# A megakernel's last stage: fifteen weight buffers instead of thirteen, in the order in which memory comes free

## The chip, the cores and the metric

The kernel runs on one core of a Trainium2 chip. The time is the device time of one execution in microseconds. The kernel before took 4176.57 us, the median of three runs (4174.07 to 4178.53).

## The reference

Thirteen layers follow each other on 512 nodes with 768 features: four mixers (linear attention of several kinds), four graph layers on a graph of 8,704 edges, and four feed-forward layers, with a residual sum between them. All numbers are float32. The change lies in the last layer, a mixture of 16 experts in which each expert chooses its nodes, with shared experts beside them. For normalised nodes `xn` (512 x 768) it computes, in the form in which the kernel does it:

```
score = sigmoid(xn @ gate_weight.T)                 # 512 x 16
for each of 16 experts e:
    the 64 nodes with the highest score[:, e]       # 64 = 512 * 2 / 16
    h = silu(xn[chosen] @ Wg[e].T) * (xn[chosen] @ Wu[e].T)      # 64 x 3072
    x[chosen] += score[chosen, e] * (h @ Wd[e].T)
x += (silu(xn @ Ws_g.T) * (xn @ Ws_u.T)) @ Ws_d.T   # shared, 1536 hidden features
```

`Wg`, `Wu` and `Wd` hold 16 x 3072 x 768 numbers each. Together they are 453 MB, and each of them is read exactly once.

## The kernel before, in words

The whole network is one program. Feature matrices lie in SBUF node-major (`xn`, 128 nodes on the partitions, four groups `t`) or feature-major (`xnT`, 128 features on the partitions, six chunks `k`). `x` holds the residual stream. PE multiplies into PSUM, whose eight banks are handed out one at a time by `ps()` (line 238).

Instructions are written as a data flow on tiles. A planner, at build time, sets the order on each engine from the order of the text and from its own estimate of when the inputs of each instruction are there; it also adds all semaphores. `tc.issue_after(i)` puts the instructions of a block behind `i` on `i`'s engine and adds no wait on another engine. A tile of a pool takes the next of the pool's buffers and waits until all readers of the tile that had it are done. A pool that is opened on memory of a closed one waits in the same way for the tiles that lay there.

**Weights** come through SP's DMA queue in tiles of 128 x 2304 numbers, 1,152 KB each, by `w` (line 254; `wk` and `wr` are views of it). SP issues them strictly in order. No more than eight of these loads are under way at once, since each has one of eight semaphores. Up to the last stage they go through a pool `wp` of six buffers at the right end of SBUF. Small rows (biases) have a pool `rowp` beside it.

**The stage before** is `last_two` (line 1643): mixer and graph layer run interleaved. The mixer reads six qkv weight tiles (`m3_wqkv`) and then two projection tiles (`m3_wp`); the projection at line 1694 reads the tile `qk` and adds into `x`. As soon as a group of nodes is done, `norm1` normalises it into `xn`, and POOL writes it to memory as `there`, from which the experts' rows are fetched later. `to_fm` with `cut` (line 357) then transposes `xn` into `xnT`, three groups first and the last one when it is ready. The normalising square root on ACT (line 404) is kept as `self.root`.

**The last stage** is `ffn3` (line 1814).

- Line 1825 closes `wp` and `rowp`, and line 1826 opens a pool of 13 weight buffers, `f3_w`. By the sizes of the pools below it, this pool begins 64 bytes short of a multiple of 512 bytes, and so does each of its buffers.
- Experts are worked on in pairs `q` (eight of them), and each pair's 3072 hidden features in eight blocks `n` of 384. This makes 64 steps. A step `(q, n)` needs six weight tiles: two of `Wg` and two of `Wu` for `up` (line 1975) and two of `Wd` for `down` (line 1988). The two experts of a pair sit on 64 columns of PE each, side by side.
- The main loop (line 2039) does `up` of the next step and `down` of this one. `down` transposes `h` into `hT` and adds into two PSUM banks. After the last block of a pair they are copied to `outs`.
- `beside` spreads all other work over the steps: ranking the next pair (`rank`), choosing and fetching its rows (`choose`, `fetch`, `turn`), the way back (`way` makes the weighted selection `ohT`, `back` adds the outputs into `x`), and the twelve units of the shared experts (`shared`, `shared_down`). A unit of shared weights is three tiles `sw` of 384 KB that POOL loads into a pool of six buffers.
- The first pair has no earlier step to hide behind. Its ranking is `first_rank` (line 1859), once for each expert: PE spreads the scores over the partitions, ACT counts greater ones through `Sign` with an accumulator, and DVE counts equal ones in the right order. Then `shared(0, 0)`, `choose(0)`, `fetch(0)`, `shared(0, 1)` and `turn(0)` lead to the first `up`.

The mixtures `f0` and `f2` earlier in the network (`moe`, line 815) load their gate weights `wg` on ACT's queue at their own start (line 826).

Of the kernel before, what the change touches and what calls it, by code (L numbers as in the profile page):

```python
# [21 lines left out]
P = 128  # L22
# [148 lines left out]
class Net:  # L171
    def __init__(self, ctx, tc, dram, at, out):
        self.tc, self.nc, self.d, self.at, self.out = tc, tc.nc, dram, at, out
        nc = self.nc
        self.cw = ExitStack()
        self.wp = self.cw.enter_context(tc.tile_pool(name="wp", bufs=6, side="right"))
        self.keep = ctx.enter_context(tc.tile_pool(name="keep", bufs=1))
        self.small = ctx.enter_context(tc.tile_pool(name="small", bufs=4))
        self.rowp = self.cw.enter_context(tc.tile_pool(name="rowp", bufs=2, side="right"))
# [87 lines left out]
    def wk(self, ap):  # L267

        return self.w(ap).rearrange("p (k n) -> p k n", k=KC)
# [87 lines left out]
    def to_fm(self, x, out, cut=0):  # L357

        if cut:
            ps = [self.ps() for _ in range(KC)]  # L360
            for t in range(cut // P):
                for f in range(KC):
                    self.tr(ps[f][:, t * P : (t + 1) * P], x[:, t, f * P : (f + 1) * P])
            for f in range(KC):
                self.copy(out[:, f, :cut], ps[f][:, :cut])
            for f in range(0, KC, 3):
                p = self.ps()
                for k in range(3):
                    self.tr(p[:, k * P : (k + 1) * P], x[:, NT - 1, (f + k) * P : (f + k + 1) * P])
                self.copy(out[:, f : f + 3, cut:], p[:, :HW].rearrange("p (k n) -> p k n", k=3))  # L370
            return
        ps = [self.ps() for _ in range(KC)]
        for t in range(NT):
            for f in range(KC):
                self.tr(ps[f][:, t * P : (t + 1) * P], x[:, t, f * P : (f + 1) * P])
        for f in range(KC):
            self.copy(out[:, f, :], ps[f])

# [16 lines left out]
    def norm1(self, x, out, t):  # L395
# [10 lines left out]
        nc.vector.tensor_scalar(out[:, t, :], x[:, t, :], mv[:, 0:1], r, OP.subtract, OP.mult)  # L406
# [408 lines left out]
    def moe(self, f, act, xn, xnT, bs=None, fill=None, later=None):  # L815
# [6 lines left out]
        with ExitStack() as c:  # L822
            one = c.enter_context(tc.tile_pool(name=f + "_one", bufs=1))
            two = c.enter_context(tc.tile_pool(name=f + "_two", bufs=2))
            wg = one.tile([P, KC, 32], F32, name="wg")
            nc.scalar.dma_start(wg.rearrange("p k e -> p (k e)"), d[f + "_wg"])
# [987 lines left out]
    def ffn3(self, xnT, gate, there):  # L1814
# [5 lines left out]
        with ExitStack() as c:  # L1820
            two = c.enter_context(tc.tile_pool(name="f3_two", bufs=2))
            one = c.enter_context(tc.tile_pool(name="f3_one", bufs=1))
            sp = c.enter_context(tc.tile_pool(name="f3_s", bufs=6))

            self.cw.close()
            self.wp = c.enter_context(tc.tile_pool(name="f3_w", bufs=13))

            first = self.small.tile([P, 1], F32, name="r3")
            with self.tc.issue_after(self.root):
                nc.scalar.activation(first, self.eps, AF.Sigmoid)  # L1830
            io = one.tile([P, P], F32, name="io")
            nc.gpsimd.iota(io, pattern=[[1, P]], base=0, channel_multiplier=0, allow_small_or_imprecise_dtypes=True)
            number = self.number
            above = one.tile([P, NT, NX], F32, name="above")
            counted = one.tile([P, NX, NT, 3], F32, name="counted")
# [5 lines left out]
            side = one.tile([P, 7 * P], BF16, name="side")  # L1841
# [4 lines left out]
            loT = one.tile([P, N], F32, name="loT")  # L1846
# [12 lines left out]
            def first_rank(e):  # L1859
                p = self.ps()  # L1860
                for t in range(NT):
                    self.tr(p[:, t * P : (t + 1) * P], sc[:, t, e : e + 1].to_broadcast([P, P]))
                for t in range(NT):
                    junk = one.tile([P, N], BF16, name="sign")
                    i = nc.scalar.activation(junk, p, AF.Sign, scale=BIGGER, bias=low[:, t, e : e + 1],  # L1865
                                             accum_out=signs[:, t, e : e + 1])
                    junk = one.tile([P, N], BF16, name="junk")
                    nc.vector.scalar_tensor_tensor(junk, p, sc[:, t, e : e + 1], side[:, (3 - t) * P : (7 - t) * P],  # L1868
                                                   OP.is_equal, OP.mult, accum_out=sides[:, t, e : e + 1])
                return i  # L1870

            def rank(e):
# [4 lines left out]
                for t in range(NT):  # L1877
                    s = sc[:, t, e : e + 1]
                    for n, (a, b, op) in enumerate(((0, t * P, OP.is_ge), (t * P, N, OP.is_gt))):
                        if a < b:  # L1880
                            junk = one.tile([P, N], BF16, name="junk")
                            nc.vector.tensor_scalar(junk[:, a:b], p[:, a:b], s, None, op, OP.add,
                                                    accum_out=counted[:, e, t, n : n + 1])
                    junk = one.tile([P, N], BF16, name="junk")
                    nc.vector.scalar_tensor_tensor(junk[:, :P], p[:, t * P : (t + 1) * P], s, before, OP.is_equal, OP.mult,
                                                   accum_out=counted[:, e, t, 2:3])
                nc.vector.tensor_reduce(above[:, :, e : e + 1], counted[:, e], AX.X, OP.add)
# [3 lines left out]
            def choose(q):  # L1891

                oh = two.tile([P, NT, 2, CAP], BF16, name="oh")
                chosen[q] = oh, two.tile([P, KC, P], F32, name="xg")
# [4 lines left out]
            rows = {}  # L1899

            def fetch(q):
# [4 lines left out]
                sums = two.tile([P, 1], F32, name="sums")  # L1906
                nc.vector.tensor_reduce(sums, p[:, :2], AX.X, OP.add)
                who = two.tile([P, 1], I32, name="who")
                nc.vector.tensor_copy(who, sums)
# [35 lines left out]
            def shared(u, b):  # L1945
# [10 lines left out]
                if b == 0:  # L1956
                    nc.scalar.activation(h, p, AF.Silu)
                else:
                    nc.vector.tensor_mul(h, h, p)
# [199 lines left out]
```

## Time and profile before

| what | us |
| --- | --- |
| median of three runs | 4176.57 |
| the profiled execution, its own time | 4179.75 |
| its span | 4177.7 |
| first load of an expert weight issued | 3043.68 |
| first expert matmul | 3075.92 |
| last load of an expert weight landed | 4164.0 |
| PE busy, of the span | 4027.0 |
| expert matmuls, line 1981 | 567.6 |
| expert matmuls, line 1997 | 322.5 |

The profile is of one execution. Times in it are microseconds from the start of its span; the durations of single groups in the page are in nanoseconds. PE is the matrix engine and PEld its weight loads, DVE the vector engine, ACT the scalar engine, and POOL and SP issue DMAs here; POOL computes a little as well. A name like `SPq` is an engine's queue. `L1981` is line 1981 of the kernel before, and `ps<-w,xg` says that a matmul wrote PSUM from the tiles `w` and `xg`. A matmul in float32 appears as two records. The mean granted clock of PE over the execution was 0.989 of full speed.

### The profile page before, as it was taken

To read this page: it belongs to the slowest core of one execution; us is meant where nothing else is said; L and a number is where in the kernel's file an instruction comes from. 1 tells how busy PE (TensorE), PEld (TensorE's weight loads), DVE (VectorE), ACT (ScalarE), POOL (GpSimd) and SP (SyncE) were. 2 spreads that over 40 slices of the span, in tenths; PEclk is the share of its full clock that TensorE was granted. 3 is DMA by queue.
4 is the path that set the end of the run, shared out by engine and by line. 5 is a ranking of instruction groups with operands and counts; after the bars stand their busy time and mean duration, and the time that the engine had idled before them with its cause. 6 is when DMAs were issued, how large, how long until landed. Compare 5 with 4: busy or idle time off the path is not lost. (4 is left out here: it accounts for less than half of the span.)

```text
span 4177.7 us, 39229 instructions
## 1 busy us (share of the span) xinstructions
PE 4027.0 (96%) x16020; PEld 2066.7 (49%) x16061; DVE 1214.8 (29%) x2899; ACT 648.5 (16%) x1222; POOL 274.4 (7%) x329
## 2 busy tenths in 40 slices
PE   8989999999999999999999999999989999999998
PEld 3444555554455667655544444454644444444443
DVE  7721211113332147313411111126832122212211
ACT  1212000012222216311101010024510000000000
POOL 1120000010031010000000000020200000000000
PEclk9999999999999999999999999999999999999999
DMA  3210011121184011302211111082099999999998
GB/s 124 71 69 34 35 63 51 53 78 36 62 312 143 23 70 46 132 25 78 98 46 57 46 61 42 3 325 82 15 373 422 421 421 421 421 422 421 422 422 361
DMA packets 99548, 710.89 MB, mean 170 GB/s; under 512 B 12608, under 2 KB 12944, under 8 KB 29984
## 3 DMA queue, kind: packets, MB, share of 16 engines
q1 hardware_dynamic: 78064, 601.20, 36.0%
q0 software_dynamic: 16816, 95.80, 6.1%
q10 hardware_dynamic: 4480, 11.28, 0.7%
q8 instruction: 131, 2.15, 0.2%
q14 instruction: 57, 0.47, 0.0%
HBM read 685.68 MB, written 22.54 MB: 170 GB/s over the span
## 5 line engine op out<-in xcount | busy, mean ns | idle before, releaser
L1981 PE MATMUL ps<-w,xg 128*64 128x384 f32 x3072 | 567.6, 489 | 5.3 <-DMA w<-in_f_Wg_dram 3.0
L1981 PEld LDWEIGHTS ps<-w,xg 128*64 128x64 f32 x3072 | 235.3, 137 | 293.1 <-issue 264.1
L1601 PE MATMUL ps<-aT,w 128*128 128x512 f32 x864 | 372.3, 592 | 0.0
L1997 PE MATMUL ps<-w,hT 128*64 128x384 f32 x1536 | 322.5, 490 | 6.3 <-DMA w<-in_f_Wd_dram 2.9
L334 PE MATMUL ps<-xnT,w 128*128 128x512 f32 (+1 forms) x732 | 322.8, 598 | 0.2 <-ACT xnT L252 0.2
L1601 PEld LDWEIGHTS ps<-aT,w 128*128 128x128 f32 x864 | 164.2, 190 | 203.6 <-issue 202.3
L334 PE MATMUL ps<-w,xnT 128*128 128x384 f32 x672 | 222.7, 488 | 0.0
L334 PEld LDWEIGHTS ps<-xnT,w 128*128 128x128 f32 (+1 forms) x732 | 134.7, 185 | 176.3 <-issue 172.7
L1997 PEld LDWEIGHTS ps<-w,hT 128*64 128x64 f32 x1536 | 132.5, 136 | 171.8 <-issue 146.5
L411 DVE TENSOR_TENSOR x<-x,ps 128x384 f32<-128x384 f32 x224 | 123.4, 553 | 263.7 <-PE ps L334 193.0
L334 PE MATMUL ps<-C,parts 128*128 128x512 bf16 x843 | 187.8, 380 | 3.5 <-DVE inv L1623 2.4
L334 PE MATMUL ps<-w,hT 128*128 128x384 f32 x552 | 184.6, 490 | 2.6 <-ACTq L1056 1.7
L334 PEld LDWEIGHTS ps<-w,xnT 128*128 128x128 f32 x672 | 127.7, 191 | 88.8 <-issue 5.8
L1611 DVE TENSOR_TENSOR aT<-inv,ps 128x512 f32<-128x512 f32 x72 | 49.4, 686 | 365.7 <-PE ps L334 365.7
L1984 ACT ACTIVATE h<-ps 128x384 f32<-128x384 f32 x64 | 31.4, 490 | 788.9 <-PE ps L1981 788.9
L516 PE MATMUL ps<-ohd,so 128*128 128x512 bf16 x533 | 128.4, 391 | 21.1 <-DVE so L513 20.4
L1985 DVE TENSOR_TENSOR h<-h,ps 128x384 f32<-128x384 f32 x64 | 35.4, 554 | 376.8 <-PE ps L1981 376.8
L334 PEld LDWEIGHTS ps<-w,hT 128*128 128x128 f32 x552 | 103.1, 190 | 80.1 <-ACT xbT L252 7.1
L334 PE MATMUL ps<-w,aT 128*128 128x384 f32 (+1 forms) x416 | 139.6, 486 | 0.5 <-DVE aT L250 0.4
L334 PE MATMUL ps<-xnT,sw 128*128 128x512 f32 x288 | 139.6, 616 | 0.0
L334 PEld LDWEIGHTS <-parts 128*128 128x128 bf16 x864 | 84.8, 98 | 108.1 <-issue 8.9
L334 PE MATMUL ps<-w,nodesT 128*128 128x384 f32 x384 | 129.1, 486 | 0.0
(507 smaller groups left out, 4634.7 us busy)
## 6 DMA issues: line engine op xcount, KB each, us to landing
w<-in_f_Wg_dram SPq DMA_DIRECT2D x128, 1152.0 KB, 22.2
w<-in_f_Wu_dram SPq DMA_DIRECT2D x128, 1152.0 KB, 22.2
w<-in_f_Wd_dram SPq DMA_DIRECT2D x128, 1152.0 KB, 22.2
w<-in_g_w_dram SPq DMA_DIRECT2D x54, 1152.0 KB, 5.2
w<-in_m_wqkv_dram SPq DMA_DIRECT2D x24, 1152.0 KB, 7.5
w<-in_g_t_dram SPq DMA_DIRECT2D x12, 1152.0 KB, 5.1
w<-in_m_wp_dram SPq DMA_DIRECT2D x8, 1152.0 KB, 5.1
ea<-in_edge_attr_dram SPq DMA_DIRECT2D x34, 256.0 KB, 2.7
```

The lines of the kernel that those rows point to most:

```text
L334: i = self.nc.tensor.matmul(out, a, b, start=n == 0, stop=n == len(pairs) - 1)
L411: self.nc.vector.tensor_add(xs, xs, p)
L516: nc.tensor.matmul(p, so[:, n, t * P : (t + 1) * P], ohd[:, j, :], start=j == 0, stop=j == EJ - 1)
L1601: nc.tensor.matmul(outs[nb * 3 + f], w[:, k, f * P : (f + 1) * P], xT[:, k, :], start=first and k == 0, stop=last and k == KC - 1)
L1611: nc.vector.tensor_mul(aT[:, f, :], inv[:, r, :], p)
L1981: nc.tensor.matmul(p[a * 64 : a * 64 + 64, :HW], xg[:, k, a * CAP : (a + 1) * CAP], ws[b][a][:, k, :], start=k == 0, stop=k == KC - 1)
L1984: nc.scalar.activation(h, pg[:, :HW], AF.Silu)
L1985: nc.vector.tensor_mul(h, h, pu[:, :HW])
L1997: nc.tensor.matmul(po[nb][a * 64 : a * 64 + 64, :HW], hT[:, f * P + a * 64 : f * P + a * 64 + 64], wd[a][:, f, nb * HW : (nb + 1) * HW], s ...
```

## The change

- The ring of weight buffers has 15 places instead of 13, in four pools, and tile `i` takes its place by `i % 15`: places 0 to 3, 9 and 10 are the six old buffers of `wp`, which stays open; 4 to 8 are a pool `early`; 11 and 12 a pool `tail`; 13 and 14 a pool `rest_` that takes `rowp`'s memory.
- All weight buffers begin on a multiple of 512 bytes. A pad of 480 bytes at the right end of SBUF (`edge`, which POOL clears at the start) and one of 64 (`room`) see to it.
- The tiles `oh`, `xg`, `rows`, `ohT` and `hs` lie in a pool `late`, opened first and so in the place of `xn`. To make room `hs`, `ohT`, `outs`, `hT` and `who` have one buffer instead of two, `sw` five instead of six, `counted` two experts instead of 16, and several early tiles share memory with later ones.
- `first_rank` becomes `first_ranks`: both experts at once, ACT on one PSUM bank and DVE on the other, then the other way round.
- `shared(0, 1)` is cut in the middle of its six products, and `fetch(0)` stands between its halves. `shared_down(0, ...)` follows at once, ahead of the main loop. `way(q)` moves by two steps. The sum in `fetch` writes integers itself.
- `to_fm` with `cut` becomes `to_fm_last`, which says which copies ACT and DVE do and places DVE's behind the last normalising. The early table load of `Sigmoid` on ACT goes behind ACT's last copy instead of behind the square root.
- The gate weights of the mixtures `f0` and `f2` are loaded before `moe` is called, on POOL's queue, into a pool of the caller.

```diff
         self.cw = ExitStack()
+        edge = self.cw.enter_context(tc.tile_pool(name="edge", bufs=1, side="right"))
+        nc.gpsimd.memset(edge.tile([P, 120], F32, name="edge"), 0.0)
         self.wp = self.cw.enter_context(tc.tile_pool(name="wp", bufs=6, side="right"))
...
-        self.rowp = self.cw.enter_context(tc.tile_pool(name="rowp", bufs=2, side="right"))
+        self.cr = ExitStack()
+        self.rowp = self.cr.enter_context(tc.tile_pool(name="rowp", bufs=2, side="right"))
...
+    def gate_of(self, pool, f):
+        t = pool.tile([P, KC, 32], F32, name=f + "_gate")
+        self.nc.gpsimd.dma_start(t.rearrange("p k e -> p (k e)"), self.d[f])
+        return t
...
+    def to_fm_last(self, x, out):
+        nc, cut = self.nc, (NT - 1) * P
+        ps = [self.ps() for _ in range(KC)]
+        for t in range(NT - 1):
+            for f in range(KC):
+                self.tr(ps[f][:, t * P : (t + 1) * P], x[:, t, f * P : (f + 1) * P])
+        for f in (0, 1, 3, 4):
+            i = nc.scalar.copy(out[:, f, :cut], ps[f][:, :cut])
+        with self.tc.issue_after(self.scaled):
+            for f in (2, 5):
+                nc.vector.tensor_copy(out[:, f, :cut], ps[f][:, :cut])
+        for f in range(0, KC, 3):
...
-            wg = one.tile([P, KC, 32], F32, name="wg")
-            nc.scalar.dma_start(wg.rearrange("p k e -> p (k e)"), d[f + "_wg"])
...
+            late = c.enter_context(tc.tile_pool(name="f3_late", bufs=2))
             two = c.enter_context(tc.tile_pool(name="f3_two", bufs=2))
             one = c.enter_context(tc.tile_pool(name="f3_one", bufs=1))
-            sp = c.enter_context(tc.tile_pool(name="f3_s", bufs=6))
-            self.cw.close()
-            self.wp = c.enter_context(tc.tile_pool(name="f3_w", bufs=13))
+            tail = c.enter_context(tc.tile_pool(name="f3_m", bufs=2))
+            sp = c.enter_context(tc.tile_pool(name="f3_s", bufs=5))
+            c.callback(self.cw.close)
+            early = c.enter_context(tc.tile_pool(name="f3_w", bufs=5))
+            self.cr.close()
+            rest_ = c.enter_context(tc.tile_pool(name="f3_r", bufs=2))
+            self.taken = 0
+            def ring():
+                i, self.taken = self.taken % 15, self.taken + 1
+                return self.wp if i < 4 or 9 <= i < 11 else early if i < 9 else tail if i < 13 else rest_
...
+            def first_ranks():
+                ps = [self.ps() for _ in range(2)]
+                for e in range(2):
+                    for t in range(NT):
+                        self.tr(ps[e][:, t * P : (t + 1) * P], sc[:, t, e : e + 1].to_broadcast([P, P]))
+                for e in range(2):
+                    for t in range(NT):
+                        junk = two.tile([P, N], BF16, tag="h", name="sign")
+                        i = nc.scalar.activation(junk, ps[e], AF.Sign, scale=BIGGER, bias=low[:, t, e : e + 1],
+                                                 accum_out=signs[:, t, e : e + 1])
+                    for t in range(NT):
+                        junk = one.tile([P, N], BF16, name="junk")
+                        j = nc.vector.scalar_tensor_tensor(
+                            junk, ps[1 - e], sc[:, t, 1 - e : 2 - e], side[:, (3 - t) * P : (7 - t) * P],
+                            OP.is_equal, OP.mult, accum_out=sides[:, t, 1 - e : 2 - e])
+                return i, j
...
-            def shared(u, b):
+            def shared(u, b, between=None):
...
+                for k in range(KC):
+                    with tc.issue_after(i.ins) if i else nullcontext():
+                        i = nc.tensor.matmul(p, w[:, k, :], xnT[:, k, :], start=k == 0, stop=k == KC - 1)
+                    if between and k == KC // 2 - 1:
+                        with tc.issue_after(i.ins):
+                            i = between()
...
-                beside[8 * q + 2].append((way, q))
+                beside[8 * q + 4].append((way, q))
...
             with tc.issue_after(last.ins):
-                last = fetch(0)
+                last = shared(0, 1, lambda: fetch(0))
             with tc.issue_after(last.ins):
-                shared(0, 1)
+                for t in range(NT):
+                    shared_down(0, t)
             turn(0)
```

## The prediction

> **What bounds the kernel now.** I began with the time strip of the page: from the 30th of 40 slices on, the DMA engines stand at 9 tenths and move 421 to 422 GB/s, and PE stands at 9 too. So the last quarter, the stage that the change rewrites, is full on two resources at once. The table by stretches says the same in numbers (columns: stretch, length, busy time and count of PE, PEld, DVE, ACT, POOL, then granted clock, DMA share, GB/s):
>
> ```profile
> 3000.00:3050.00 50.00, 48.36 (x239) 32.70 (x238) 29.11 (x64) 15.37 (x27) 10.69 (x20) 1.00 0.31 110
> 3050.00:3100.00 50.00, 40.33 (x185) 18.80 (x185) 18.23 (x59) 10.16 (x23) 2.15 (x3) 0.90 1.01 418
> 3500.00:3600.00 100.00, 99.38 (x500) 44.28 (x496) 20.36 (x55) 6.03 (x12) 2.63 (x4) 1.00 1.01 422
> ```
>
> Before 3050 the DMA is nearly idle; afterwards it never rests. The list of what the load queue waited for between 2850 and 3082 us says why it starts so late (columns: waits in total, times, longest):
>
> ```profile
> SPq L258 <- DVE x L1796: 128.0, 1, 128.0
> SPq L258 <- PE ps L334: 78.8, 3, 41.5
> SPq L258 <- PE ps L1981: 14.5, 1, 14.5
> ```
>
> SP waits for memory: 128.0 us for the last addition of the graph layer, at about 3022, then for the last matmul of the mixer's projection, until the first load goes at 3043.68. Having filled 13 buffers it waits 14.5 us, from 3065.5 to 3080.0, for PE to finish with the first one.
>
> Which of the two bounds decides? I set each of the 384 weight loads' landing against the first matmul that uses it. Tile 6 landed 19.6 us before its use, tile 60 11.9 us, tile 144 5.4 us, tile 242 0.03 us, and from tile 368 on all wait. PE therefore begins with a stock, eats it for 700 us, scrapes the bottom near 3760, 3900 and 4037 and runs dry at 4122. The end shows it (start, length, instruction, in brackets the idle time before it):
>
> ```profile
> 4130.63 4.09 PE L1981 MATMUL ps<-w,xg 128*64 128x384 f32 x24 [1.49 <-DMA w<-in_f_Wg_dram]
> 4136.20 3.76 PE L1981 MATMUL ps<-w,xg 128*64 128x384 f32 x21 [1.01 <-DMA w<-in_f_Wu_dram]
> 4141.77 3.12 PE L1997 MATMUL ps<-w,hT 128*64 128x384 f32 x17 [0.83 <-DMA w<-in_f_Wd_dram]
> ```
>
> All such waits from 4122 on add up to 0.40+1.49+1.01+0.83+1.47+1.01+0.21+1.21 = 7.6 us. Both bounds must fall for the time to fall. Last I read the start of the stage:
>
> ```profile
> 3052.80 5.32 PE L334 MATMUL ps<-xnT,sw 128*128 128x512 f32 x12
> 3063.95 0.75 DVE L1868 SCALAR_TENSOR_TENSOR junk<-ps,sc,side 128x512 bf16<-128x512 f32 x1 [0.85 <-ACT sign L1865]
> 3065.43 0.75 PE L334 MATMUL ps<-number,oh 128*128 128x2 bf16 x4 [7.31 <-issue]
> 3066.04 8.20 PE L334 MATMUL ps<-xnT,sw 128*128 128x512 f32 x12
> 3074.72 0.87 PE L355 MATMUL ps<-ident,rows 128*128 128x128 f32 x6 [0.48 <-DMA rows<-f_there,who]
> 3075.92 7.96 PE L1981 MATMUL ps<-w,xg 128*64 128x384 f32 x48 [0.32 <-DVE xg L250]
> 3084.30 2.75 PE L334 MATMUL ps<-sw,hs 128*128 128x384 f32 x8
> ```
>
> PE has nothing for 7.31 us while ACT and DVE rank the first two experts, then computes the second half of shared unit 0 while the rows are fetched. The first expert matmul is at 3075.92; call that T0.
>
> **The change part by part.**
>
> *First ranks.* ACT and DVE took turns on the same PSUM bank, eight pairs from 3052.57 to 3064.71. The change gives each its own bank and lets them swap. The slower is DVE: 4 times about 0.8 us (0.75 and the read of the accumulator), twice, with a hand-over: 6.7 us from 3052.7, so 3059.4 instead of 3064.7, 5.3 us less. Then as before 0.4 for the sums and 0.9 for the one-hots: 3060.7. The separate cast (0.15 us) goes.
>
> *Order on PE.* Unit 0's first product ends at 3058.1, half of the second (2.66) at 3060.8, the matmuls of fetch follow (0.75), then the other half: 3064.2. The gather is issued at about 3062; with the 7.5 us that it took here under full DMA it lands at 3069.5, sooner if the queue is empty. Meanwhile PE does unit 0's down products, two groups like the one of 2.75 us, 5.5 us, after 0.8 us for the product on DVE: 3070.5. Turn 0.87 and copy 0.3: T0 is about 3071.5, **4.4 us earlier**. The down products formerly ran after T0: **5.5 us** of PE work leaves the stretch that PE fills without a pause.
>
> [...] The stretches of the clock:
>
> ```profile
> 3052.80:3058.20 5.40, 5.32 (x14) 2.10 (x12) 2.28 (x6) 2.84 (x8) 0.00 (x0) 1.00 1.01 428
> 3065.40:3074.30 8.90, 8.78 (x16) 3.62 (x16) 1.45 (x6) 0.43 (x1) 1.04 (x1) 0.65 1.01 419
> ```
>
> The same 12 matmuls take 5.32 us at clock 1.00 and 8.20 at 0.65, after the idle 7.31: 2.9 us lost. [...]
>
> *The loads.* Tiles 0 to 3 of the ring go to the old weight pool, whose buffers come free as blocks 2 to 5 of the mixer's qkv weights are done, at 2917, 2941, 2969 and 2996 by the trace. Tiles 4 to 8 lie where the graph layer lay (free at 3022), tiles 9 to 14 where the projection's weights, the qk tile and the bias rows lay (3043). Each tile takes 2.79 us when loads queue up, so nine are in by about 3042, with the first shared weights, and all 15 by about 3062. Before, about 10 tiles had landed at 3080.0, when PE gave back the first buffer, and 374 followed in 1084 us, to 4164.0. After, PE gives back the first at T0 + 4.1 = 3075.6 with 15 landed; 369 follow in 1084 - 5 x 2.79 = 1070 us, and the restart from an empty queue costs 5.2 - 2.8 = 2.4 us: the last lands at 4148. From there to the end 13.7 us as now: **4161.7 by DMA**.
>
> *By PE*: 4177.7 - 4.4 - 5.5 - 7.6 (waits that the stock now covers) = **4160.2**. The two nearly meet; the later decides, 4161.7.
>
> *Buffers on 512 bytes.* In the packet records a row of 9216 bytes takes a median of 349 ns in this stage, against 347 in the first MoE's gather and in loads to the old pool. [...] The loads to the old pool were off the line as well and yet took 347, so I take 2 in 349, at most 6 us, and as PE then decides at 4160.2 only 1.5 of it. Lower bound 0.
>
> *Gates of the other two MoEs.* They move from ACT's queue (0.35 us each) to POOL's (0.54), to an earlier place. POOL had been idle there for 46.8 us. In the first MoE this was late:
>
> ```profile
> 1160.24 3.59 PE L342 MATMUL ps<-xnT,wg 128*32 128x512 f32 x12 [2.20 <-DMA wg<-in_f_wg_dram]
> ```
>
> The last copy of xnT ends at 1159.4, and the first is ready by 1158.2, so 0.8 to 2.2 us come back, more if the clock stays up (3.59 us against 1.91 for such a group at full clock); the ranking on DVE behind it sets the gather. I take 1.5. In the second MoE, PE waited for xnT: 0.
>
> *Fewer buffers* for hT, outs, ohT, hs and who: 0. The next hT is copied about 5 us after PE's last use of the old one (3516.65 and 3521.5 in one step), which is the cover; without it each step would pay a copy of about 0.5 us, 32 us in all. For ohT the later place of way is the cover. Five shared buffers instead of six: POOL already waits 728.9 us for them, a whole unit ahead; the gathers behind these waits on POOL's queue come after the same PE work as before. Last-stage norm and copies: ACT's table load moves behind its copies, 0 to 0.3. The pad's memset at the start: 0.2 us on POOL, 0.
>
> **Sum** against the execution's own span: 4177.7 to 4160.2 (the DMA bound less 1.5 for the packets) less 1.5 for the first MoE: 4158.7, 19.0 us less. I keep 17, because two bounds that meet never fit step by step. The profiled execution's own time is 4179.75 (2.05 around its span), 3.2 above the median of 4176.57; the median less 17 is **4159.5**.
>
> **Rivals.**
>
> *The order on PE gets worse (slower).* PE's order is fixed at build time by a planner that guesses when loads arrive. Where it guesses late, it parts a pair of matmuls that would run side by side:
>
> ```profile
> 3499.74 4.73 PE L1981 MATMUL ps<-w,xg 128*64 128x384 f32 x26
> 3504.77 4.08 PE L1981 MATMUL ps<-w,xg 128*64 128x384 f32 x22
> ```
>
> That is 8.67 us on the chain instead of the 7.96 at 3075.92: about 0.65 us a break. Another plan could have more of them. Of 192 places (three pairs of tiles in 64 steps) perhaps half are broken now; to be slower by 0.2% the plan needs (17 + 8.4) / 0.65 = 39 more, then 4186. For: the plan is new from T0 on. Against: a fuller ring should make the planner wait less. Chance 0.12.
>
> *The loads don't start earlier (no change).* If one wait ahead of tile 0 on SP is still the projection's, the stream starts at 3043.7 as now, is never interrupted, and ends at 4164 whatever PE does: 4177.7 - 1.5, or 4175 on the median. SP is in order, so tile 4's memory at 3022 can hold back 9 to 14 too, without harm. With half of the early tiles: 4168. Against it: the blocks' ends at 2917 to 2996. Chance 0.13.
>
> *Both bounds fall further.* [...] Chance 0.11.
>
> **How the numbers follow.** The main forecast has 0.64, its own range 4151 to 4168. A change of 0.2%, 8.4 us, is about what a measurement of this kernel can tell from none. Faster: 0.64 + 0.11 = 0.75; same 0.13; slower 0.12. The range from 4149 to 4176 leaves out the slower rival and the low tail, some 0.17.
>
> **What would show it.** First ring loads at about 2917, 2941, 2969, 2996, five at 3022; DMA idle between about 3062 and 3075; no PE gap near 3060 and clock 1.00; T0 near 3071.5; first waits for weights later than 4122 or none. It is wrong if the stock is as small as before when the stream becomes steady, or if expert matmuls take more time in total than now.

## The result

The kernel after takes 4144.89 us (median of 4 runs, 4142.03 to 4147.45); the kernel before, run beside it, 4177.55 (4 runs, 4174.07 to 4179.18). The ratio is 0.9921, 95% interval 0.9908 to 0.9934. It is faster by 32.7 us. The forecast had the direction right and the gain at half its size: 17 us, 4159.5, with a range that ended at 4149.

The profiled execution of the kernel after spans 4142.6 us, 35.1 less than that of before. Its table by stretches, in the columns known from before (stretch, length, busy time and count of PE, PEld, DVE, ACT, POOL, granted clock, DMA share, GB/s):

```profile
3000.00:3050.00 50.00, 48.06 (x221) 30.92 (x221) 27.55 (x64) 16.39 (x38) 9.68 (x18) 1.00 0.70 284
3050.00:3100.00 50.00, 47.94 (x225) 21.68 (x225) 21.52 (x74) 4.47 (x8) 3.41 (x5) 1.00 0.83 332
3500.00:3600.00 100.00, 100.00 (x542) 45.10 (x542) 17.52 (x40) 6.04 (x12) 2.64 (x4) 1.00 1.01 427
```

Two things differ. The DMA is at work before 3050 (284 GB/s instead of 110) and rests afterwards; and when both kernels are in their steady state, at 3500, the same loads run at 427 GB/s instead of 422. What the load queue waited for between 2850 and 3082 (total, times, longest):

```profile
SPq L262 <- PE ps L338: 175.0, 8, 41.3
SPq L262 <- PE ps L2024: 40.7, 3, 28.7
SPq L262 <- DVE x L1814: 26.0, 1, 26.0
```

The wait of 128.0 us for the graph layer is 26.0 now. Single tiles go at 2908.9, 2932.7, 2960.0 and 2987.8, five at 3014.4 to 3016.5, six more up to 3036.9; then SP waits 28.7 us, to 3066.0, until PE gives back the first buffer. By the packet records all 15 tiles have landed when the first expert matmul begins; in the kernel before it was 9.7 of 13. The start of the stage:

```profile
3043.72 7.89 PE L1995 MATMUL ps<-xnT,sw 128*128 128x512 f32 x18
3051.45 0.40 PE L338 MATMUL ps<-number,oh 128*128 128x2 bf16 x4
3051.71 2.82 PE L1995 MATMUL ps<-xnT,sw 128*128 128x512 f32 x6
3055.38 5.43 PE L338 MATMUL ps<-sw,hs 128*128 128x384 f32 x16 [0.85 <-DVE hs L2002]
3060.64 0.82 PE L359 MATMUL ps<-ident,rows 128*128 128x128 f32 x6
3061.92 7.96 PE L2024 MATMUL ps<-w,xg 128*64 128x384 f32 x48 [0.46 <-DVE xg L254]
```

The gap of 7.31 us is gone, and 18 matmuls at a granted clock of 1.00 (3043.7 to 3051.4) fill its place. The end has two waits for weights instead of eight, 2.5 us instead of 7.6:

```profile
4112.28 4.09 PE L2024 MATMUL ps<-w,xg 128*64 128x384 f32 x24 [1.42 <-DMA w<-in_f_Wg_dram]
...
4117.94 3.76 PE L2024 MATMUL ps<-w,xg 128*64 128x384 f32 x21 [1.10 <-DMA w<-in_f_Wu_dram]
```

**Where the 35.1 us lie.** The work ahead of the last stage takes a time that differs by several us from run to run: the last matmul of the projection (the one that adds its bias; call its start P) lies at 3043.3 in the kernel before, but at 3033.4 in e6_start below, whose code is the same up to there. So two intervals are read instead of the span. From P to the end: 4177.7 - 3043.28 = 1134.4 us before, 4142.6 - 3034.74 = 1107.9 after, **26.5 less**. This interval repeats well: a second kernel with the last stage of before gives 1134.6, one with the stage of after in another load order 1108.1. And at the gate of the first MoE, from the start of the last six transposes of xn to the end of the gate product: 6.2 to 6.9 us in the seven kernels of this study with the old gate (6.7 in the profile before), 3.4 in all seven with the new one, **about 3 less**. The rest, some 5 us of the spans or 3 of the medians, is within the spread of the work ahead of P, so it is not counted as a gain of the change.

### The profile page after: what moved, and what is told of

The parts are those of the page before. It is cut to its first block, busy times and chain, and to the rows that moved or that the text cites. A ratio compares the mean times of both kernels' runs of the same rounds, so it can differ in the third digit from the quotient of the medians.

```text
span 4142.6 us, 39287 instructions
## 1 busy us (share of the span) xinstructions
PE 4014.0 (97%) x16061; PEld 2065.4 (50%) x16061; DVE 1212.9 (29%) x2890; ACT 648.9 (16%) x1223; POOL 276.7 (7%) x331
```

## The experiments

All times are medians, each beside runs of the kernel before on the same chip. "Landed" is the landing of the last weight tile, counted from P; "tail" is from there to the end of the span.

| kernel | us | before beside it | ratio, 95% interval | P to end | landed | tail |
|---|---|---|---|---|---|---|
| before | 4177.55 | | | 1134.4 | 1120.3 | 14.1 |
| after | 4144.89 | 4177.55 | 0.9921 (0.9908, 0.9934) | 1107.9 | 1093.8 | 14.1 |
| e1_align | 4166.92 | 4176.69 | 0.9974 (0.9963, 0.9985) | 1124.7 | 1108.2 | 16.6 |
| e2_nopads | 4161.31 | 4176.69 | 0.9965 (0.9952, 0.9979) | 1122.9 | 1108.7 | 14.2 |
| e4_ring13 | 4150.07 | 4176.69 | 0.9940 (0.9926, 0.9953) | 1113.4 | 1099.3 | 14.1 |
| e5_order | 4144.58 | 4176.69 | 0.9921 (0.9908, 0.9935) | 1108.1 | 1094.0 | 14.1 |
| e3_gates | 4169.29 | 4173.93 | 0.9993 (0.9984, 1.0002) | 1134.6 | 1120.3 | 14.3 |
| e6_start | 4171.83 | 4173.93 | 0.9996 (0.9987, 1.0005) | 1134.3 | 1120.2 | 14.1 |
| e1b_256 | 4162.57, one run | 4173.93 | | 1123.0 | 1107.8 | 15.2 |
| e1c_480 | 4173.20, one run | 4173.93 | | 1137.3 | 1123.2 | 14.1 |
| e7_both | 4162.72 | 4177.69 | 0.9964 (0.9951, 0.9978) | 1119.3 | 1105.3 | 14.0 |
| e1d_128 | 4174.84, one run | 4177.69 | | 1133.9 | 1119.8 | 14.2 |
| e9_late | 4179.79 | 4177.85 | 1.0005 (0.9995, 1.0014) | 1142.3 | 1128.2 | 14.1 |
| e10_noedge | 4148.55 | 4177.85 | 0.9926 (0.9909, 0.9943) | 1110.4 | 1096.3 | 14.1 |

The last column is worth more than it seems. In twelve of the fourteen the end follows the last landing by 14.0 to 14.3 us, the time that PE needs for what still hangs on the last tile. In those kernels the loads set the end. Only in e1_align (16.6) and its twin e1b_256 (15.2) had PE still other work to do when the last tile came.

**e1_align: the ring on 512 bytes, alone.**

```diff
 number = self.number
+one.tile([P, 16], F32, name="room")
 above = one.tile([P, NT, NX], F32, name="above")
```

> The kernel before with one unused tile of 64 bytes ahead of the ring's pool, so that the ring's buffers begin on a multiple of 512 bytes instead of 448 past one; nothing else. Theory (the beginning of the buffer sets the rate of the loads): loads at 427 GB/s instead of 422 between 3100 and 4100 us, the 9216-byte packet records near 348 ns in the mean instead of 352, the waits for weights after 4122 us gone or nearly so; PE's own work then bounds the stretch, so 6 to 12 us less than before. The prediction's term: 0 to 6 us less, 1.5 likeliest. Rival (the rate comes from the order of the loads, not from where the buffers begin): 422 GB/s still, and the time within 2 us of before.

Measured: 9.8 us less in the median, 9.7 from P to the end. The mean 9216-byte record from 3100 to 4100 takes 348.7 ns instead of 351.9. No wait for weights is left on PE, and the load queue spends its time differently. Its waits from 3060 to 4180 in the kernel before, and then in e1_align:

```profile
SPq L258 <- PE ps L1981: 273.5, 119, 14.5
SPq L258 <- DMA w<-in_f_Wg_dram: 188.1, 87, 4.8
SPq L258 <- DMA w<-in_f_Wu_dram: 166.4, 80, 3.7
SPq L258 <- DMA w<-in_f_Wd_dram: 164.3, 78, 3.9
SPq L258 <- PE ps L1997: 141.0, 64, 7.4
```

```profile
SPq L258 <- PE ps L1982: 601.2, 213, 15.6
SPq L258 <- PE ps L1998: 299.4, 115, 7.5
...
SPq L258 <- DMA w<-in_f_Wg_dram: 7.3, 3, 3.3
```

Before, SP waited 518.8 us for earlier loads and 414.5 for buffers; now it waits 900.6 us for PE to give buffers back. So the bound went from the loads to PE, and 1124.7 us is what PE needs with the old start of the stage.

The gain is larger than the visible waits. The steps of the two kernels begin at the same times after T0, to 0.02 us, up to the one at 817.8 us, so the pad makes nothing faster on PE itself. From there the kernel before falls behind by 10.0: by 1.1 at a stop of 0.27 us at 3904.3, which the prediction did not list, and by the rest at its eight stops from 4122 on. At each of these nine stops the matmul ahead runs out its full 0.49 us, where in an unbroken row the next one starts after 0.16 (48 of them take 7.96): 9 x 0.33 = 3.0, and with the waits of 7.9 us that is 10.9, near the 10.0. The theory holds; the prediction's term (1.5, at most 6) does not.

**e2_nopads: the kernel after without both pads.**

```diff
-edge = self.cw.enter_context(tc.tile_pool(name="edge", bufs=1, side="right"))
-nc.gpsimd.memset(edge.tile([P, 120], F32, name="edge"), 0.0)
...
-one.tile([P, 16], F32, name="room")
```

> The kernel after without its two pads (the 480-byte one at the right edge and the 64-byte one of the last stage): the five buffers of the early pool begin 448 past a multiple of 512 and those of the old weight pool 480 past one, as they did before. Theory: 422 GB/s again, and since the last loads of the kernel after land with 0 to 5 us to spare, the time rises by 8 to 12 us to about 4155. The prediction's term: 1.5 us more, at most 6. Rival (where buffers begin does nothing): within 2 us of the kernel after.

Measured: 16.4 us more than after in the median, 15.0 from P to the end; mean record 352.5 ns. The DMA summary from 3100 to 4100 of the kernel after, of e1_align and of e2_nopads:

```profile
DMA packets 53124, 426.96 MB, mean 427 GB/s; under 512 B 6125, under 2 KB 6125, under 8 KB 8238
```

```profile
DMA packets 52975, 425.18 MB, mean 425 GB/s; under 512 B 6126, under 2 KB 6126, under 8 KB 8366
```

```profile
DMA packets 52391, 420.58 MB, mean 421 GB/s; under 512 B 6063, under 2 KB 6063, under 8 KB 8239
```

426.96 to 420.58 is 1.5%. A tile of 128 rows of 9216 bytes takes 2.76 us at 427 GB/s, 384 of them 1060 us, and 1.5% of that is 16: the 15 us measured. (The 425 of e1_align is no slower DMA: it paused for buffers.) The theory said 8 to 12; it took the waits at the end for all the slack that would be lost, where in truth the loads are the bound throughout. This is the part of the gain that the forecast had counted at only 1.5 us: without the pads the kernel takes 4161.3, within 2 us of the forecast. That it comes so near is partly luck, since other terms were off too, in both directions (see below).

**e1b, e1c, e1d: which boundary?** The pad of e1_align with 320, 32 and 192 bytes, so that the ring begins 256, 480 and 128 past a multiple of 512.

```diff
-one.tile([P, 16], F32, name="room")
+one.tile([P, 80], F32, name="room")
```

(80 floats in e1b_256, 8 in e1c_480, 48 in e1d_128.)

> As the aligned version of before, but with 320 bytes of padding: the ring begins 256 past a multiple of 512. Theory 1 (what counts is a multiple of 512): 9216-byte records near 352 ns, 422 GB/s, as before. Theory 2 (what counts is a multiple of 256): near 348 ns, 425 to 427 GB/s, time near 4167. Theory 3 (only a multiple of 64 or less counts): would also hold for before, so no difference from it.

> As the aligned version of before, but with 32 bytes of padding: the ring begins 480 past a multiple of 512, where the old weight pool of the kernel before lies. If the prediction was right that loads to such a place run like aligned ones: near 348 ns and 425 to 427 GB/s. If it merely saw them under a lighter load: 352 ns or more in the mean, 422 GB/s or less.

> As the aligned version of before, but with 192 bytes of padding: the ring begins 128 past a multiple of 512. So far the mean 9216-byte record took 348.7 ns at 0, 348.8 at 256, 351.9 at 448 (192 past a multiple of 256) and 353.4 at 480 (224 past one). If the cost grows with the bytes past a multiple of 256: 350 to 351 ns here, 423 to 425 GB/s. If any start off a multiple of 256 costs the same: 352 to 353 ns, 421 to 422 GB/s. If 128 is enough: 348 to 349 ns.

The DMA summary from 3100 to 4100 of e1b_256 and of e1c_480:

```profile
DMA packets 52978, 425.20 MB, mean 425 GB/s; under 512 B 6126, under 2 KB 6126, under 8 KB 8366
```

```profile
DMA packets 52372, 420.31 MB, mean 420 GB/s; under 512 B 6070, under 2 KB 6070, under 8 KB 8254
```

Mean record and rate by where the ring begins: 0 past 348.7 ns, 256 past 348.8 ns (both 425 GB/s, limited by PE); 128 past 352.0 ns and 422; 448 past (before) 351.9 and 422; 480 past 353.4 and 420. So a multiple of 256 was enough here. Where a ring of thirteen on the line (a multiple of 512) is not held back by PE (e7_both), the mean is 347.5 ns; against that, a start off the multiple costs 1.3, 1.3 and 1.7%. It hardly grows with the bytes past it (128, 192, 224), so of the two descriptions in the last expectation the second is nearer. Each of the three places was run once, but the records behind a mean number over 44,000.

**e10_noedge: only the old pool off the line.**

```diff
-edge = self.cw.enter_context(tc.tile_pool(name="edge", bufs=1, side="right"))
-nc.gpsimd.memset(edge.tile([P, 120], F32, name="edge"), 0.0)
```

> The kernel after without the pad at the right edge alone: the six buffers of the old weight pool lie 480 past a multiple of 512, the other nine stay on one. From the last matmul of the projection to the end: after 1107.9 us, without both pads 1122.9. If each tile pays for where its own buffer begins: the six of fifteen take 353 ns a record, the others 347, 424 GB/s over all and 5 to 7 us more than after. If one misplaced pool slows all queues: near 1121. If the old pool's place does nothing, as the prediction held: 1108.

Measured: 2.5 us more than after from P to the end, mean record 348.3 ns, 426 GB/s: none of the three. Six of fifteen buffers lie 480 past the line, yet 91% of the records take 347 ns as if all were aligned. When all thirteen lay there (e1c_480), 6% did. The cost is therefore no fixed price of a record here. The packet records tell more when they are sorted by start and cut into tiles. The share of records of 350 ns or more, by place in the ring (0 to 3, 9 and 10 are the six off the line; the first 60 tiles are left out):

| place | 0 | 1 | 2 | 3 | 4 | 5 | 6 to 8 | 9 | 10 | 11 | 12 to 14 |
|---|---|---|---|---|---|---|---|---|---|---|---|
| % | 1 | 13 | 36 | 45 | 31 | 4 | 0 | 1 | 2 | 3 | 0 to 1 |

In a run of four loads off the line the slow records grow from tile to tile, and they are gone within two tiles on the line; a run of two shows hardly any. So in this kernel the time of a load hangs on the loads just ahead of it, and not only on where its own buffer begins. What lies behind that, no run shows.

**e4_ring13: two buffers fewer.**

```diff
-rest_ = c.enter_context(tc.tile_pool(name="f3_r", bufs=2))
-    i, self.taken = self.taken % 15, self.taken + 1
-    return self.wp if i < 4 or 9 <= i < 11 else early if i < 9 else tail if i < 13 else rest_
+    i, self.taken = self.taken % 13, self.taken + 1
+    return self.wp if i < 4 or 9 <= i < 11 else early if i < 9 else tail
```

> The kernel after with a ring of thirteen: the pool of two that takes the place of the bias rows is left out, all else is the same. Theory (the loads bound the end, so the stock at the start of the stage counts in full): two tiles of 2.76 us fewer are in when PE gives back the first buffer, so 5.5 us more than after, about 4150. Rival (PE's own work bounds it, the stock is ample): within 2 us of after, 4143 to 4147.

Measured: 5.5 us more from P to the end, 5.2 in the median. Two tiles are 2 x 2.76 = 5.5. Each of these two tiles, in hand before PE gives the first one back, counts in full.

**e5_order: the same buffers in the opposite order.**

```diff
-    return self.wp if i < 4 or 9 <= i < 11 else early if i < 9 else tail if i < 13 else rest_
+    return tail if i < 2 else rest_ if i < 4 else early if i < 9 else self.wp
```

> The kernel after with the same fifteen buffers taken in the opposite order, those that come free last first: no load can then start before about 3034 us, and fifteen tiles of 2.76 us take until about 3076. Theory: the loads never pause between 3034 and the end; the pause that the kernel after has before 3066 us, some 10 to 14 us, is lost, the end comes 8 to 12 us later, about 4154; the first expert matmul stays at 3062. Prediction's bound by loads said the same thing in its own numbers. Rival (PE bounds it): within 2 us of after.

Measured: no difference, 4144.58 us and 1108.1 from P. The edit did not hold the loads back as it was meant to. Its load queue (start, length, instruction):

```profile
2913.04 0.33 SPq L262 DMA_DIRECT2D w<-in_f_Wd_dram  x1
...
3018.53 0.80 SPq L262 DMA_DIRECT2D w<-in_f_Wg_dram  x2
```

A down tile goes first, at 2913. The planner sorts the loads by when their memory comes free, so the early start is the same, only with other tiles. So what counts is which memory the fifteen buffers use; the order in which the ring is written to run through them is worth nothing here.

**e9_late: the first fifteen loads held back.**

```diff
...
 i = self.nc.sync.dma_start(t[:parts, :n], ap)
+self.hold -= self.hold > 0 and (self.tc.add_manual_dep(i.ins, self.added.name, mybir.DependencyInfo(mybir.DependencyClass.Sync, mybir.DependencyReason.DATA), reason="late start") or 1)
...
-self.nc.vector.tensor_add(xs, xs, p)
+self.added = self.nc.vector.tensor_add(xs, xs, p).ins
...
-self.taken = 0
+self.taken, self.hold = 0, 15
```

> The kernel after with one wait more: the first fifteen loads of the ring wait for the last addition of the projection, so that none starts before the place where the loads of the kernel before began; ring, pads and the start of the stage are those of after. The planner, told of the wait, parts more pairs of expert matmuls while the loads are young. From the last matmul of the projection to the end the kernel after takes 1107.9 us. Theory (the loads bound the end, so each tile that is not in when PE gives back the first buffer costs its 2.76 us): about 11 of 15 tiles in, 8 to 11 us more, 1116 to 1119. Rival (the early start only fills buffers that PE does not need yet): 1108 to 1110.

Measured: all of the gain is gone, 4179.79 us and 34.4 us more from P. The wait sits later than intended, for by the time the loads are written down the last addition is that of shared unit 0's down products:

```profile
3064.46 0.80 SPq L261 DMA_DIRECT2D w<-in_f_Wg_dram  x2
```

That is 26.7 us after P, so 0 tiles are in where the kernel after has 15. The arithmetic still fits: 15 x 2.76 = 41.4 us of loading ahead, less the time that the kernel after stands still from there to its first free buffer (it goes on at 3066.03, 31.3 after P: 4.6 us), is 36.8 against 34.4 measured. Here the loads never pause: 26.7 from P to the first issue, 1101.5 to the last landing and a tail of 14.1 make up the 1142.3. PE waits 24.5 us for weights:

```profile
PE ps L2024 <- DMA w<-in_f_Wg_dram: 16.8, 9, 6.2
PE ps L2040 <- DMA w<-in_f_Wd_dram: 4.0, 6, 0.8
PE ps L2024 <- DMA w<-in_f_Wu_dram: 3.7, 7, 1.0
```

The 22 stops cost their lost overlap too: 24.5 + 22 x 0.33 = 31.8 us, against 2.5 + 0.7 in the kernel after. The 6 us that are left over on PE's side were not taken apart.

**e6_start: the new start of the stage alone.**

```diff
-rest = pieces[2:]
+rest = pieces[4:]
-for e in range(2):
-    last = first_rank(e)
+last, _ = first_ranks()
...
-    last = fetch(0)
+    last = shared(0, 1, lambda: fetch(0))
 with tc.issue_after(last.ins):
-    shared(0, 1)
+    for t in range(NT):
+        shared_down(0, t)
```

The definitions of `first_ranks` and of `shared` are those of the change.

> The kernel before with only the start of the last stage changed: each of the first two experts ranked in a bank of its own, the gather between the halves of shared unit 0's second product, and the unit's down products ahead of the first expert matmul. Theory: the first expert matmul comes 5 to 6 us earlier; the loads, which bound the end, stay as fast and only get their first buffer back 5 to 6 us earlier, so the end comes 5 to 6 us earlier, about 4171, and PE waits some 5 us more for weights near the end, where the moved products of 5.5 us now leave room. Rival (PE bounds the end): both terms count, 10 to 11 us less, about 4166. Rival (loads bound it and their start at 3043.7 decides): no change.

Measured: nothing, 1134.3 us from P against 1134.4. The third account is right: the loads bind, and their start decides. By the packet records they take 1119.8 us from the first issue to the last landing, in the kernel before 1119.9, and they never pause. When PE gives back its first buffer, 10.3 tiles of 13 have landed (11.0 before), so others are still under way, and a buffer that comes free earlier brings no load forward. T0 itself came 2.3 us earlier (30.4 after P instead of 32.6), less than the 5 to 6 expected: the rows were late behind the loads (1.41 us). PE waits for weights 14.6 us instead of 7.9.

**e7_both: the pad of e1_align and the new start of e6_start.**

```diff
+one.tile([P, 16], F32, name="room")
 above = one.tile([P, NT, NX], F32, name="above")
```

With it go all the edits of e6_start.

> The kernel before with the pad of 64 bytes and the new start of the last stage together; the ring keeps its thirteen buffers and its late start. From the last matmul of the projection to the end: before 1134.4 us, with the pad alone 1124.7, with the start alone 1134.3, after 1107.9. Theory (the loads hid what the start gains; once they are faster, PE bounds the stage and the start counts): 1113 to 1117, so 8 to 11 us less than with the pad alone; what is left to 1107.9, 6 to 9 us, is the earlier and larger stock. Rival 1 (the loads bound it again at once): 1120 to 1124. Rival 2 (the earlier stock does nothing): 1108 to 1110.

Measured: 1119.3 us from P, between the theory and the first rival: 5.4 less than with the pad alone, of 8 to 11 expected. PE's waits show why (3060 to 4180):

```profile
PE ps L2009 <- DMA w<-in_f_Wd_dram: 2.7, 3, 1.2
PE ps L1993 <- DMA w<-in_f_Wg_dram: 1.5, 1, 1.5
PE ps L1993 <- DMA w<-in_f_Wu_dram: 1.4, 3, 0.9
```

5.6 us of waits for weights are back and the tail is 14.0: as soon as PE had room the loads were the bound again, at their faster rate. From here to the kernel after it is another 11.4 us. Two tiles are 5.5 of them (e4_ring13); the other 5.9 are the earlier start of the loads together with all else that e7_both leaves out, not parted further.

**e3_gates: the gates alone.**

```diff
-wg = one.tile([P, KC, 32], F32, name="wg")
-nc.scalar.dma_start(wg.rearrange("p k e -> p (k e)"), d[f + "_wg"])
...
-net.moe("f0", AF.Gelu, xn, xnT, "f0_bs", fill=part)
+net.moe("f0", AF.Gelu, xn, xnT, net.gate_of(right, "f0_wg"), "f0_bs", fill=part)
```

The same is done for `f2`.

> The kernel before with the gate weights of the first and second MoE loaded from GpSimd's queue before the MoE begins, as the kernel after does; nothing else. Theory (the gate was late by more than the wait of 2.2 us shows, because the product also ran at a lowered clock): the gate product takes 2.25 us instead of 3.59 and starts 3 to 5 us earlier against the work before it, the last stage begins 4 to 5 us earlier, and all of it reaches the end, since both the loads and PE of the last stage move with it: 4172. The prediction's term: 1.5 us less, 4175. Rival (it is swallowed by the gather behind it): within 1 us of before.

```profile
1157.06 2.25 PE L342 MATMUL ps<-xnT,f_wg_gate 128*32 128x512 f32 x12 [0.24 <-DVE xnT L250]
```

The gate product takes 2.25 us instead of 3.59 (there at a granted clock of 0.52, 1160.24 to 1163.83) and waits no longer for its weights; from the start of the last six transposes of xn to its end 3.4 us instead of 6.7. The last stage is unchanged. In the total, 4169.29 beside 4173.93, the interval of the ratio reaches from 0.9984 to 1.0002, so the runs show the local gain and do not settle how much of it arrives.

## Where the prediction held and where it failed

The path was right: the loads bind, and an early stock shortens it. Two terms of the sum failed. The one for buffers on 512 bytes was held at 1.5 us where the runs show 9.7 to 15.0, and the bound by PE, which was the reason for holding it there, was too high.

**The loads' early start** was right in time and number: tiles at the blocks' ends, five at the graph layer's end, all 15 in before the first expert matmul, the queue idle until PE gives back a buffer (predicted T0 + 4.1, measured 3066.03 - 3061.92 = 4.1). e4_ring13 and e9_late bear out the price per tile.

**Order on PE and first ranks.** T0 counted from P came 5.5 us earlier (32.6 to 27.2), predicted 4.4. In e7_both the new start gave 4.0 of it (33.0 to 28.9); 0.5 more comes from the last norm and its copies (4.71 to 4.17 from P to the gate product, taken as 0 to 0.3); the last 1.0 was not taken apart. The granted clock is 1.00 from 3050 to 3066, where the gap was (0.65 behind it in the kernel before), and the 18 matmuls take 7.89 us, as long for each as the 12 in 5.32; so to reckon with them at that length made no error here.

**Buffers on 512 bytes: the step that failed.** It said "I take 2 in 349, at most 6 us, and as PE then decides at 4160.2 only 1.5 of it". Measured: 9.7 us when added to the kernel before, 15.0 when taken from the kernel after. Two errors are in the size, and a third, that PE decides, is the next point. The 2 in 349 compares medians; the means are 351.9 and 347.6, twice as far apart, since four in ten of the records before took 350 ns or more.

The value was then held low because of loads to the old pool, off the line and yet 347 ns. But these came almost always alone or in twos: by the packet records 104 of the 114 tiles ahead of the last stage were the first or second of a run. Twice in the same trace six follow each other without a pause, from 7.6 to 28.4 us and from 1690.0 to 1709.3, and there the fifth and sixth tiles have a median of 351 ns, with 89 to 99% of the records at 350 or more. In the kernel after, with the old pool on the line, the same tiles take 347. It is the rise that e10_noedge shows, and it stood in the trace that the prediction was read from.

In size, the means of before and after lie 1.2% apart (351.9 and 347.6 ns), the rates of after and e2_nopads 1.5% (427 and 421 GB/s); the time differs by 15 us. A beginning on a multiple of 256 was as good as one on 512 (e1b_256: 348.8 ns against 348.7). The loss does not grow in step with the bytes past that multiple: for 128, 192 and 224 bytes it was 1.3, 1.3 and 1.7% over the 347.5 of e7_both. Nor is a price per record seen (e10_noedge).

**"By PE: 4160.2": the step that failed with it.** It took the waits of 7.6 us as all that the loads cost PE. With the loads out of the way (e1_align) PE was done 9.7 us sooner. Less 5.5 for T0 and 5.5 for the moved products, that is 1113.7 from P, not the 4160.2 - 3043.3 = 1116.9 of the sum; and the kernel after is at 1107.9 with the loads still its bound, so PE alone would need less than that.

Where the rest lies can be summed over the traces, from the start of each PE instruction to the start of the next. The expert matmuls, up and down, take 804.1 us in the kernel after, of which 2.5 + 0.7 are late weights, and 806.0 in e1_align, which has none: about 5 us less. All other work of PE behind T0 takes 271.8 instead of 279.4, where 5.5 was counted. Why the expert matmuls take less is open. The planner's order differs, so fewer parted pairs could be the reason. But the count of expert matmuls that start close ahead of the next one does not settle it: within 0.1 us they are 2136 of 4608 against 2170 in e1_align, within 0.2 us 2223 against 2170. No run changed the order alone. The result, 4144.89, lies below 4151, where the main forecast's own range ends, on the side of the rival "both bounds fall further" (chance 0.11). For the loads the runs show where it comes from, 15.0 us by the pads (e2_nopads); for PE's bound they do not.

**By DMA** the sum put the last landing at 4148, 1104.7 after P. Without the pads it was 1108.7, with them 1093.8. The mechanism was right to 4 us; the rate was the error. Of the 4 us some 2.5 are a miscount: at 3080.0 the kernel before had 10.9 tiles in by the packet records, not "about 10", so the stock grew by 4.1 tiles and not by 5.

**Gates**: 1.5 predicted, about 3 measured at the place. The wait went from 2.2 to 0.24 us, and the product behind it from 3.59 to 2.25; the second part was seen and left out of the value taken.

**Fewer buffers, five shared buffers, the pads' own cost**: 0 predicted; nothing in the traces speaks against it, and none was tried alone.

**The rivals.** The slower one (a worse order on PE) did not come. The one without change would have needed loads that start as late as before: e6_start has them, and there the new start of the stage gained nothing; with the pad as well (e7_both) it was 15.1 us. e9_late holds the loads back 26 us longer than that rival meant, so it is no test of it.

## What to carry to other kernels

When two bounds lie close together, a change to one may be worth nothing alone (e6_start, 0.1 us) and count only once the other has moved (e7_both, 5.4), so each is summed for itself and the later one decides; here the time from the last landing to the end showed which one it was. Visible waits understated here what late loads cost, since each stop also lost the overlap of the two matmuls around it, 0.33 us. In a stretch where the DMA is full, look at the mean of the packet records (351.9 against 347.6 ns here), not the median alone (349 against 347), and at where the buffers begin: 64 bytes of padding were worth 9.7 us here. A place that looks harmless in single loads (347 ns here) has not been seen under a steady stream (353.4 in e1c_480).

## What the runs showed of the hardware that was not expected

- Where the SBUF buffers of the ring begin changed the rate of saturated loads. The mean 9216-byte record from 3100 to 4100 us took 347.5 ns in e7_both, 347.6 in after, 348.7 in e1_align and 348.8 in e1b_256, where all of them begin on a multiple of 256 bytes; off it, it took 351.9 in before, 352.0 in e1d_128 and 353.4 in e1c_480. The rate was 427 GB/s in after, against 422, 422 and 420 in the last three.
- The place of the buffer did not set the time of a load alone. In the kernel before, loads to the old pool had a median of 347 ns where they came singly, and of 351 as the fifth and sixth of an unbroken row. In e10_noedge, with six of fifteen buffers off the line, the share of records of 350 ns or more was 1, 13, 36 and 45% in four such tiles in a row, then 31, 4 and 0% in the next ones on the line; the mean was 348.3.
- The granted clock was low after two short pauses. In e6_start PE waited 1.41 us for rows, did 0.85 us of transposes and waited another 0.32; over the next 9.7 us the clock was 0.82, and 48 matmuls took 9.65 us, where the next 48 took 7.96. In e7_both, with waits of 0.9 and 0.5 us but none for the rows, it was 1.00 from 3070.5 to 3078.5. That the pauses are the cause was not shown. The table by stretches of e6_start:

```profile
3063.70:3073.40 9.70, 9.64 (x49) 3.92 (x50) 0.00 (x1) 0.74 (x2) 0.00 (x0) 0.82 1.01 421
```
